# A sparse power-attention and expert layer on one core: relu sums on VectorE, expert tiles in two halves, and a new plan

## The chip, the core and the metric

The kernel runs on one core of a Trainium2 chip. The core has a matrix engine (TensorE, "PE" in the rows), a vector engine (VectorE, "DVE"), an activation engine (ScalarE, "ACT"), a general engine (GpSimd, "POOL") and a queue engine that issues transfers (SyncE, "SP"). TensorE writes its results into PSUM, which has 8 banks of 128 x 512 float32; VectorE and ScalarE read them from there, GpSimd does not. The metric is the device time of one execution in microseconds; the median of several executions counts.

## What is computed

The input x has 4 sequences of 1024 tokens with 128 channels. All arithmetic is in float32.

```
xn = layernorm(x)
out = x + attention(xn) + experts(xn)

attention:  q, k, v = split(xn @ W_attn + b_attn)        # 16 heads of 8
            s = q k^T;  s = s - mean(s over all keys)
            s = s / (mean |s| over all keys + 1e-6) * gain
            r = max(s where key <= query else -1000, 0) ** 4
            y = (r / (sum r + 1e-6)) v;  out = y @ W_proj + b_proj
experts:    two best of 8 experts per token (softmax of their two gate logits)
            h = (x w1 + b1) * (x w2 + b2);  g = silu(h wg + bg);  y = g w3 + b3
```

The mean of |s| runs over all 1024 keys, the fourth power over the causal ones only.

## The kernel before, in words

**Attention.** Each sequence is cut into two chunks of 512 queries (c = 0, 1); the 16 heads are taken in 4 groups of 4 (r). Matmuls of 4 heads run side by side in four 32-row or 32-column strips of the array. For the mean of |s|, `up` (L942) scores queries against keys to the right, and DVE (L955) or ACT (L957) adds up absolute values, one bank each. For the attention proper, `score` (L1066) writes scores of one block of 128 keys against 512 queries into 4 banks, one for each head. Then a relu on ACT (L1092) or DVE (L1094) moves each bank into an SBUF tile `u1`; a block on the diagonal is first masked by DVE (L1085). Two squarings (L1117 on ACT, L1119 on POOL, 1024 wide for two heads) make the fourth power in `u`. TensorE takes two products of them into one accumulator bank: `relus` (L1133) with the constant selector `pick`, which adds up the relus over the keys (with that sum, and the sum of all signed scores, the absolute values over the causal keys are found without a second pass), and `values` (L1142) with the values V and a column of ones. A sequence's second chunk has 4 whole blocks of keys ahead of its diagonal groups, the first chunk has none.

**Experts.** Token copies are scattered by an indirect transfer on POOL's queue (L723) into rows of a table `xs`, sorted by expert and padded to tiles of TS = 256 rows: 39 tiles. For each tile SP loads its rows and the weights of its expert (L1234 to L1238, 640 KB of weights), TensorE transposes the rows (L1247), multiplies by w1 and w2 (L1257), wg (L1264) and w3 (L1273); ACT adds the first bias (L1331) and takes the silu (L1363), DVE multiplies the two halves (L1339) and weights the result (L1285), and POOL adds the rows to a table in memory by an indirect transfer (L1293), 128 rows each.

**The order.** Every engine executes a fixed list. A planner in the kernel (`Plan.run`) makes the lists: each step has an engine or a choice of engines with a cost in microseconds, the steps it depends on, the buffers it takes and gives back, and a due time (`rank`). It takes the step that can start first, after shifts by name (`SOONER`, `RANK`). Where it foresees TensorE idle for over 0.3 us while an accumulator is open, it puts in a filler matmul of zeros (`pads`, emitted at L1426).

Buffers of note: 8 PSUM banks, 6 tiles `u1`, 8 tiles `u`, 14 tiles `blk` of 1040 columns, 2 weight tiles `w`, 3 row tiles `xg`.

Of the kernel before, what the change touches and what calls it, by code (L numbers as in the profile page):

```python
# [8 lines left out]
F32 = mybir.dt.float32  # L9
# [7 lines left out]
P = 128  # L17
# [6 lines left out]
CH = 512  # L24
VE = D + 2
VW = NH * VE + 22
TS = 256
# [24 lines left out]
class Plan:  # L52
# [6 lines left out]
    SOONER = {"score": 0.23, "mask": 0.1, "norm": 0.19, "tbias": -0.09, "count": -0.58, "v": 0.01, "top": 0.2, "wT": -0.06, "kappa": -0.11, "gateT": 0.12, "k": 0.21, "abs": -0.69, "ys": -0.51, "stats": 0.59, "exp": 0.14, "sq": -0.86, "bound": 0.53, "proj": -0.42, "least": 1.02, "xg": -0.51, "give": -0.32, "yT": -0.16, "sum": -0.3, "heads": 0.32, "gate": -0.5, "headsT": 0.15, "normal": 0.19, "second": -0.02, "relu": -0.88, "y@DVE": -0.32, "gate@DVE": 0.11, "relu@DVE": 0.45, "xT": 0.46, "xg@DVE": -0.05, "relu@ACT": 0.42, "out": -0.77, "yT@DVE": -0.19, "xT@DVE": -0.19, "place": -0.11, "gate@ACT": -0.01, "g": -0.01, "wT@ACT": 0.34, "heads@DVE": -0.33, "mean": -0.33, "y": -0.03, "abs@DVE": 0.6, "ys@DVE": -0.15, "sq@ACT": -0.11, "warm": 0.63, "xg@ACT": -0.83, "norm@ACT": 0.05, "up": 0.16, "q": 0.06, "blocks": -0.09, "ys@ACT": 0.01, "spill": -0.53, "weight": -0.46, "wT@DVE": 0.22, "gain": -0.07, "gates": 0.91, "av": -0.1}  # L59
    RANK = {"score": 221, "proj": -10, "yT": -194, "xg": -11, "sums": 48, "h": -24, "tbias": -35, "bound": -15, "top": 4, "headsT": 187, "spill": 12, "blocks": 240, "place": 4, "sum": -136, "std": -27, "gateT": 10, "count": -34, "scatter": 85, "xT": 210, "y": 196, "exp": 27, "second": -251, "load": 209, "relu": -111, "keys": 126, "mask": 6, "rows": -13, "scale": 8, "turn": 101, "wT": 23, "fill": 17, "ys": -19, "bias": -6, "g": -103, "give": -106, "gate": 36, "absq": 16, "norm": -137, "warm": -16, "v": -15, "hot": -162, "gates": 21, "stats": 20, "up": 78}  # L60
# [105 lines left out]
def layer_kernel(  # L166
# [49 lines left out]
    SB = TS // P  # L216
    N_TILES = (2 * NT + E * (TS - 1)) // TS
# [10 lines left out]
    def keep(shape, name, dtype=F32):  # L228
# [5 lines left out]
        "u": (8, [P, 2, CH]), "u1": (6, [P, 2, CH]), "blk": (14, [P, TB * WX]),  # L234
        "w": (2, [P, 2 * F + FB * F + FB * C]), "xg": (3, [P, SB, WX]), "xT": (2, [P, TS]),
        "z": (2, [P, FB, TS]), "s": (2, [P, FB, TS]), "ye": (2, [P, SB, C]),         "ys": (2, [P, CH]), "yt": (2, [P, CB, C]),
# [105 lines left out]
    tiles_f = keep([P, N_TILES], "tiles_f")  # L342
    expert_f = keep([P, 1], "expert_f")
    for t, pattern, base, cm in (
        (first, [[-1, E]], E, 0),
        (tiles_f, [[1, N_TILES]], 0, 0), (expert_f, [[0, 1]], 0, 1),
    ):
        nc.gpsimd.iota(t, pattern=pattern, base=base, channel_multiplier=cm, allow_small_or_imprecise_dtypes=True)
# [24 lines left out]
    xs = dram.tile([N_TILES * TS, WX], F32, name="xs")  # L373
# [47 lines left out]
    own = keep([E, N_TILES], "own")  # L421
    one8 = keep([P, TB], "one8")
    nc.vector.memset(one8, 1.0)
    owner = keep([P, N_TILES], "owner", I32)
    biases = keep([P, 3, FB, N_TILES], "biases")
# [130 lines left out]
    def route(rank):  # L556
# [84 lines left out]
        def owners(e):  # L641

            past = room(0, N_TILES * (E - 1)).rearrange("p (n e) -> p n e", e=E - 1)
            nc.vector.tensor_tensor(
                past, tiles_f.unsqueeze(2).to_broadcast([P, N_TILES, E - 1]),
                ends(1)[:, 1:].unsqueeze(1).to_broadcast([P, N_TILES, E - 1]), ALU.is_ge,
            )
            o0 = of_buf(k1)[:, NE + 160 : NE + 160 + N_TILES]
            nc.vector.tensor_reduce(o0, past, AX.X, ALU.add)
            nc.vector.tensor_copy(owner, o0)  # L650
            nc.vector.tensor_scalar(own, o0[:E, :], expert_f[:E, :], None, ALU.is_equal)
# [8 lines left out]
        def bias(e):  # L660
            pb = of_buf(k2)[:, : 3 * FB * N_TILES].rearrange("p (i f n) -> p i f n", i=3, f=FB)
            for i in range(3):
# [7 lines left out]
                biases.rearrange("p i f n -> p (i f n)"), of_buf(k2)[:, : 3 * FB * N_TILES]  # L670
# [72 lines left out]
    def prepare(b, cs, rank):  # L743
# [65 lines left out]
        def scale(here, bound):  # L809


            t = of_buf(aq)[:, here]
            nc.vector.tensor_scalar(
                t.bitcast(I32), bound.bitcast(I32), 0x7F800000, -0x1000000, ALU.bitwise_xor, ALU.bitwise_and
            )
            nc.vector.tensor_tensor(of_buf(qb)[:, here], of_buf(qb)[:, here], t, ALU.mult)  # L816

        sd = []
        for c in range(NC):
# [12 lines left out]
                    deps=[m, qd[c]], give=[k], rank=rank,  # L832
# [76 lines left out]
        m = add("heads", {"PE": 1.3}, heads, deps=sd + [bl], take=[sh[b]], give=[aq], rank=rank + 8)  # L909
# [10 lines left out]
    def chunk(b, c, vd, sh_done, t0, t1):  # L920
# [124 lines left out]
        for r in range(NR):  # L1045
            acc = Buf("bank")
            for j, grp in enumerate(groups):
# [29 lines left out]
                for m in range(2):  # L1077
                    u1, u = u1s[m], us[m]
                    a = []
                    for g in range(2):  # L1080
# [21 lines left out]
                        if rest:  # L1102
# [3 lines left out]
                                    give=[] if near else [k], rank=rank - 200,  # L1106
# [31 lines left out]
                def values(e, r=r, parts=parts, us=us, acc=acc, begin=False, end=False):  # L1138
# [8 lines left out]
                line["sq"] = sq1  # L1147

# [4 lines left out]
                    emit=lambda e, f=relus, s=begin and not diag: f(e, begin=s), deps=e1, took=took(counted), give=[],  # L1153
                    free=(u1s, e2), last=None, take=[acc] if begin and not diag else [],
                )
                av_job = dict(
                    acc=acc,
                    emit=lambda e, f=values, s=begin and diag, t=last: f(e, begin=s, end=t), deps=e2 + vd, took=took(w),
                    give=us, free=None, last=(r, acc) if last else None, take=[acc] if begin and diag else [],
                )  # L1160
                if begin and diag:
                    now, later = pending, [av_job, relu_job]
                else:
                    now, later = pending + ([relu_job] if counted else []), [av_job]
                    if not counted:
                        add("free", {"none": 0.0}, None, deps=e2, give=u1s)
# [48 lines left out]
    def experts(routed, ranks, stored):  # L1215
# [3 lines left out]
        tile_ = [{k: Buf(k) for k in ("w", "xg", "xT", "z", "s", "ye")} for _ in range(n_)]  # L1219

        def weights_of(i):
            w = of_buf(tile_[i]["w"])
# [4 lines left out]
        def loaded(i):  # L1227


            def load(e):  # L1230
                of_ = nc.sync.value_load(owner[0:1, i : i + 1], min_val=0, max_val=E - 1)
                this = bass.DynSlice(of_, 1)
                w1s, w2s, wgs, w3s = weights_of(i)
                nc.sync.dma_start(of_buf(tile_[i]["xg"]), slots_d[:, i * SB : (i + 1) * SB, :])  # L1234
                nc.sync.dma_start(w1s, w1[this, :, :].rearrange("e p f -> p (e f)"))
                nc.sync.dma_start(w2s, w2[this, :, :].rearrange("e p f -> p (e f)"))
                nc.sync.dma_start(wgs, wg[this, :, :].rearrange("e (k p) g -> p (e k) g", p=P))
                nc.sync.dma_start(w3s, w3[this, :, :].rearrange("e (k p) h -> p (e k) h", p=P))  # L1238

            return add(  # L1240
# [218 lines left out]
```

## Time and profile before

| | |
|---|---|
| median of 3 runs | 931.68 us (931.22 to 932.55) |
| profiled execution, its own time | 934.0 us |
| its span, first to last instruction | 932.3 us |
| mean granted TensorE clock | 0.985 |
| longest groups on TensorE (busy) | L942 188.4 us, L1066 178.9 us, L1142 165.1 us, L1133 129.1 us |
| experts on TensorE (busy) | L1264 77.1 us, L1257 74.7 us, L1273 44.9 us |
| first and last w1/w2 matmul (L1257) starts | 282.0 us; the last of L1273 at 906.5 us |
| moved by transfers | 58.63 MB, of it 117 loads of 128 KB and 39 of 256 KB for expert weights |

In a row of instruction groups, the part behind "x" is the count, then come busy time in us, the mean duration of one in ns, and the idle time of the engine ahead of them with what ended it. A float32 matmul shows as two instructions. Durations of one instruction contain the tail that the next one of the same engine overlaps, so the distance from start to start is shorter than the duration when instructions follow each other closely. In a timeline row the first number is the start, the second how long the merged group lasted.

### The profile page before, as it was taken

What the parts mean: (1) busy time and instruction counts of PE and PEld (TensorE: products, weight loads), DVE (VectorE), ACT (ScalarE), POOL (GpSimd) and SP (SyncE); (2) the same over time, 40 slices, a digit from 0 to 9 for tenths busy, and PEclk for the clock granted to TensorE, in tenths of its full rate; (3) what the DMA queues carried; (4) which work ended last, traced back from release to release, by engine and by line L of the source; (5) the groups of instructions that cost most, each with busy time, mean ns of one, the idle gap of its engine ahead of it and who ended that gap; (6) DMA issues with size and microseconds to landing.
All of it is one profiled execution on the core that took longest, in us unless ns stands there. A gap on an engine that the chain in (4) does not pass through costs nothing.

```text
span 932.3 us, 20608 instructions
## 1 busy us (share of the span) xinstructions
PE 901.4 (97%) x7517; PEld 458.4 (49%) x7517; DVE 644.5 (69%) x1616; ACT 718.1 (77%) x1564; POOL 756.1 (81%) x519
## 2 busy tenths in 40 slices
PE   6899999998999999999899999999999999999996
PEld 4455433433454545545445654454545565544443
DVE  7888856568776766666567776665666776666565
ACT  5879888897786868678757877777787868678983
POOL 4478879889676889999957887999987838899992
PEclk9999999999898999999989999999999999999999
DMA  4820000000021233233212221232322222222106
GB/s 107 333 79 22 24 21 21 22 24 21 22 80 39 48 76 78 58 68 78 63 41 54 67 57 43 60 65 59 83 63 63 56 62 59 63 59 44 41 7 187
DMA packets 66275, 58.63 MB, mean 63 GB/s; under 512 B 6463, under 2 KB 62206, under 8 KB 66174
## 3 DMA queue, kind: packets, MB, share of 16 engines
q1 hardware_dynamic: 52168, 47.67, 16.8%
q0 software_dynamic: 13280, 9.38, 7.4%
q8 instruction: 59, 0.97, 0.4%
q10 hardware_dynamic: 726, 0.27, 0.2%
q14 instruction: 42, 0.34, 0.1%
HBM read 36.90 MB, written 20.40 MB: 61 GB/s over the span
## 4 chain that ended last, share of the span: by engine, by line
PE 83%; DVE 7%; POOL 6%; issue 2%; DMA 1%; ACT 1%; SPq 0%; ACTq 0%; POOLq 0%; DVEq 0%
PE bank L942 17%; PE bank L1066 16%; PE bank L1142 14%; PE bank L1133 9%; PE bank L1264 8%; PE bank L1257 7%; PE bank L1273 4%; POOL u L1119 4%; PE bank L1010 2%; POOL xs L723 1%; PE bank L767 1%; PE bank L1247 1%; DVE blk L816 1%; PE bank L1426 1%; DMA blk<-acc 1%
## 5 line engine op out<-in xcount | busy, mean ns | idle before, releaser
L1119 POOL TENSOR_TENSOR u<-u 128x1024 f32<-128x1024 f32 (+1 forms) x324 | 582.1, 1924 | 99.4 <-ACT u L1092 62.7
L1117 ACT ACTIVATE u<-u 128x1024 f32<-128x1024 f32 (+1 forms) x316 | 298.2, 971 | 11.7 <-POOL u L1119 5.6
L955 DVE TENSOR_REDUCE asum<-bank 128x1 f32<-128x512 f32 (+3 forms) x500 | 243.0, 543 | 62.1 <-PE bank L942 61.3
L1092 ACT ACTIVATE u<-bank 128x256 f32<-128x256 f32 (+2 forms) x355 | 152.4, 492 | 71.9 <-DVE u L1085 44.0
L942 PE MATMUL bank<-blk,blk 32*128 32x512 f32 (+3 forms) x1536 | 188.4, 529 | 7.1 <-DVE blk L816 4.7
L1085 DVE SCALAR_TENSOR_TENSOR u<-bank,causal 128x256 f32<-128x256 f32 (+1 forms) x384 | 121.2, 372 | 89.6 <-PE bank L1066 70.9
L1066 PE MATMUL bank<-blk,blk 32*128 32x512 f32 (+3 forms) x1536 | 178.9, 528 | 1.0 <-DVE u L1085 0.5
L1142 PE MATMUL bank<-u,V 128*32 128x512 f32 (+3 forms) x1536 | 165.1, 501 | 1.6 <-POOL u L1119 1.3
L957 ACT ACTIVATE bank<-bank 128x512 f32<-128x512 f32 (+3 forms) x268 | 130.5, 488 | 35.1 <-PE bank L942 31.8
L1293 POOL DMA_INDIRECT acc<-ye,xg x78 | 123.0, 1577 | 36.6 <-DVE ye L1285 20.5
L1094 DVE TENSOR_SCALAR u<-bank 128x512 f32<-128x512 f32 (+2 forms) x157 | 98.9, 656 | 55.9 <-PE bank L1066 55.9
L942 PEld LDWEIGHTS bank<-blk,blk 32*128 32x128 f32 x1536 | 90.6, 185 | 86.1 <-issue 13.5
L1133 PE MATMUL bank<-u,pick 128*32 128x512 f32 (+3 forms) x1280 | 129.1, 469 | 0.0
L1066 PEld LDWEIGHTS bank<-blk,blk 32*128 32x128 f32 x1536 | 65.7, 184 | 72.5 <-issue 27.1
L1133 PEld LDWEIGHTS bank<-u,pick 128*32 128x32 f32 x1280 | 43.6, 111 | 79.3 <-issue 74.5
L723 POOL DMA_INDIRECT xs<-blk,slot x64 | 64.5, 1008 | 21.4 <-DMA xs<-blk,slot 11.2
L1264 PE MATMUL bank<-z,w 128*128 128x256 f32 x312 | 77.1, 390 | 0.0
L1142 PEld LDWEIGHTS bank<-u,V 128*32 128x32 f32 x1536 | 33.9, 108 | 83.4 <-issue 58.3
L1257 PE MATMUL bank<-xT,w 128*128 128x256 f32 x312 | 74.7, 383 | 0.0
L1264 PEld LDWEIGHTS bank<-z,w 128*128 128x128 f32 x312 | 56.1, 190 | 25.9 <-issue 8.8
L1257 PEld LDWEIGHTS bank<-xT,w 128*128 128x128 f32 x312 | 56.9, 193 | 7.7 <-DVE asum L955 1.5
L1339 DVE SCALAR_TENSOR_TENSOR z<-bank,biases,z 128x256 f32<-128x256 f32 x78 | 37.2, 478 | 30.8 <-ACT z L1331 30.7
(176 smaller groups left out, 700.5 us busy)
## 6 DMA issues: line engine op xcount, KB each, us to landing
w<-in_L_ffn_w_dram SPq DMA_DIRECT2D x117, 128.0 KB
w<-in_L_ffn_wg_dram SPq DMA_DIRECT2D x39, 256.0 KB
xs<-w SPq DMA_DIRECT2D x1, 5070.0 KB
xg<-xs SPq DMA_DIRECT2D x39, 130.0 KB
acc<-w SPq DMA_DIRECT2D x1, 2048.0 KB
blk<-acc SPq DMA_DIRECT2D x4, 512.0 KB
out_dram<-xt SPq DMA_DIRECT2D x8, 256.0 KB
xt<-in_L_attn_x_dram SPq DMA_DIRECT2D x3, 512.0 KB
```

The lines of the kernel that those rows point to most:

```text
L942: nc.tensor.matmul(of_buf(ks_[g])[:, at : at + w], of_buf(q[b])[rows_, ii * P : (ii + 1) * P], of_buf(km[b][r])[rows_, k0 : k0 + w], start ...
L955: nc.vector.tensor_reduce(to, of_, AX.X, ALU.add, apply_absolute_value=True)
L957: nc.scalar.activation(of_, of_, AF.Abs, accum_out=to)
L1066: nc.tensor.matmul(of_buf(ks_[g])[:, at : at + n], of_buf(km[b][r])[rows_, jj * P : (jj + 1) * P], of_buf(q[b])[rows_, c * CH + off : (c + ...
L1092: nc.scalar.activation(to, s_, AF.Relu)
L1117: nc.scalar.activation(to, s_, AF.Square)
L1119: (nc.vector if e == "DVE" else nc.gpsimd).tensor_tensor(to, s_, s_, ALU.mult)
L1133: nc.tensor.matmul(of_buf(acc)[32 * g : 32 * g + 32, off + lo : CH], pick, of_buf(u1s[g // 2])[:, g % 2, at + lo : at + n], start=begin, s ...
L1142: nc.tensor.matmul(of_buf(acc)[32 * g : 32 * g + 32, off:CH], of_buf(Vb[b])[:, jj, h0 : h0 + 32], of_buf(us[g // 2])[:, g % 2, at : at + n ...
L1257: nc.tensor.matmul(of_buf(k)[:, j * TS : (j + 1) * TS], wt[:, f * P : (f + 1) * P], of_buf(tile_[i]["xT"]), start=True, stop=True)
L1264: nc.tensor.matmul(of_buf(k)[:, g * TS : (g + 1) * TS], weights_of(i)[2][:, f, g * P : (g + 1) * P], of_buf(tile_[i]["z"])[:, f, :], start ...
L1293: nc.gpsimd.indirect_dma_start(out=acc_d, in_=of_buf(ye)[:, j, :], in_offset=None, compute_op=ALU.add, out_offset=bass.IndirectOffsetOnAxi ...
```

## The change

1. In a second chunk, the relus of the whole key blocks are not summed by TensorE block by block. The first block's relus stay in `u1`; for the second to fourth block VectorE reads the score bank again and adds max(score, 0) to a running sum in SBUF (`more`, a scalar_tensor_tensor of 512 columns for each of 4 heads). After the fourth block one `pick` product of the sums takes the place of four. Relu and `more` of one bank are separate steps, and the bank comes free after both. The accumulator is now begun by the values product.
2. Expert slots are padded to 128 rows (TS = 128), 72 halves in all, and two halves, each with its own expert, make one tile: 36 tiles. Matmuls by weights have 128 moving columns each; biases, product and silu are done half by half; each half loads its own 640 KB.
3. The rows of a tile are loaded by a step of their own (`rows_in`), apart from the weights (`load`). Transposing waits for the rows alone, the w1/w2 products also for the weights.
4. In the preparation of a sequence, the power-of-two scale is computed inside the PSUM bank, the queries are multiplied by it from there, and a copy step puts it into SBUF for later use.
5. `SOONER` and `RANK` have new values, `w` has 4 tiles, `blk` 11.

```diff
-TS = 256
+TS = 128
...
-    SB = TS // P
-    N_TILES = (2 * NT + E * (TS - 1)) // TS
+    SB = 2
+    TW = SB * TS
+    N_TILES = -(-((2 * NT + E * (TS - 1)) // TS) // SB)
+    N_OWN = N_TILES * SB
...
-        "u": (8, [P, 2, CH]), "u1": (6, [P, 2, CH]), "blk": (14, [P, TB * WX]),
-        "w": (2, [P, 2 * F + FB * F + FB * C]), "xg": (3, [P, SB, WX]), "xT": (2, [P, TS]),
+        "u": (8, [P, 2, CH]), "u1": (6, [P, 2, CH]), "blk": (11, [P, TB * WX]),
+        "w": (4, [P, 2 * F + FB * F + FB * C]), "xg": (3, [P, SB, WX]), "xT": (2, [P, TW]),
...
-            t = of_buf(aq)[:, here]
-            nc.vector.tensor_scalar(
-                t.bitcast(I32), bound.bitcast(I32), 0x7F800000, -0x1000000, ALU.bitwise_xor, ALU.bitwise_and
-            )
-            nc.vector.tensor_tensor(of_buf(qb)[:, here], of_buf(qb)[:, here], t, ALU.mult)
+            t = bound.bitcast(I32)
+            nc.vector.tensor_scalar(t, t, 0x7F800000, -0x1000000, ALU.bitwise_xor, ALU.bitwise_and)
+            nc.vector.tensor_tensor(of_buf(qb)[:, here], of_buf(qb)[:, here], bound, ALU.mult)
...
+                if not diag and j:
+                    for m in range(2):
+                        for g in range(2):
+                            k = ks_[2 * m + g]
+
+                            def more(e, m=m, g=g, k=k, first=j == 1, before=relus_0, sums=sums):
+                                to = of_buf(sums[m])[:, g * CH : (g + 1) * CH]
+                                nc.vector.scalar_tensor_tensor(
+                                    to, of_buf(k), 0.0, of_buf(before[m])[:, g, :] if first else to, ALU.max, ALU.add
+                                )
+
+                            a = add(
+                                "more", {"DVE": t_dve(CH)}, more, deps=[scores] + (before_ if j == 1 else [added[2 * m + g]]),
+                                take=[sums[m]] if j == 1 and g == 0 else [], rank=rank - 200,
+                                behind=[added[2 * m]] if j == 1 and g else [],
+                            )
+                            add("free", {"none": 0.0}, None, deps=[a, e1[2 * m + g]], give=[k])
...
+                if not diag:
+                    def all_relus(e, sums=sums, acc=acc):
+                        for g in range(4):
+                            nc.tensor.matmul(
+                                of_buf(acc)[32 * g : 32 * g + 32, :], pick, of_buf(sums[g // 2])[:, (g % 2) * CH : (g % 2 + 1) * CH],
+                                start=False, stop=False,
+                            )
+
+                    relu_job = None
+                    if j == c * CB - 1:
+                        relu_job = dict(acc=acc, emit=lambda e, f=all_relus: f(e), deps=list(added), took=took(CH), give=sums, free=None, last=None, take=[])
...
+            def rows_(e):
+                nc.sync.dma_start(of_buf(tile_[i]["xg"]), slots_d[:, i * SB : (i + 1) * SB, :])
...
+                for j in range(SB):
+                    n = i * SB + j
+                    of_ = nc.sync.value_load(owner[0:1, n : n + 1], min_val=0, max_val=E - 1)
...
         def up(i, f, k):
-            for j, wt in enumerate(weights_of(i)[:2]):
-                nc.tensor.matmul(
-                    of_buf(k)[:, j * TS : (j + 1) * TS], wt[:, f * P : (f + 1) * P], of_buf(tile_[i]["xT"]), start=True, stop=True
-                )
+            for m in range(2):
+                for j in range(SB):
+                    nc.tensor.matmul(
+                        of_buf(k)[:, m * TW + j * TS : m * TW + (j + 1) * TS], weights_of(i, j)[m][:, f * P : (f + 1) * P],
+                        of_buf(tile_[i]["xT"])[:, j * TS : (j + 1) * TS], start=True, stop=True,
+                    )
```

## The prediction, made before the changed kernel ran

> **What bounds the kernel now.** I read the busy times first, then the groups by form, TensorE's timeline, the waits, and the busy times by stage.
>
> ```profile
> PE 901.4 (97%) x7517; PEld 458.4 (49%) x7517; DVE 644.5 (69%) x1616; ACT 718.1 (77%) x1564; POOL 756.1 (81%) x519
> ```
>
> TensorE is busy for all but 31 us of 932.3; no other engine passes 81%. The chain of work that ended last is 83% PE. So work taken off TensorE should pay, as long as no other engine takes its place. The timeline of a second chunk (start, length) gives the price of a burst of 8 instructions as distance from start to start:
>
> ```profile
> 407.62 1.16 PE L1273 MATMUL bank<-w,s 128*128 128x128 f32 x8
> 408.61 1.89 PE L1257 MATMUL bank<-xT,w 128*128 128x256 f32 x8
> 410.43 0.71 PE L942 MATMUL bank<-blk,blk 32*128 32x256 f32 x8
> 411.08 1.07 PE L1142 MATMUL bank<-u,V 128*32 128x512 f32 x8
> 411.96 1.04 PE L1133 MATMUL bank<-u,pick 128*32 128x512 f32 x8
> 412.93 1.14 PE L942 MATMUL bank<-blk,blk 32*128 32x512 f32 x8
> ```
>
> A values burst followed by a selector burst lasts 0.88 us (411.08 to 411.96); the selector burst, followed by a burst of another kind, 0.97. The groups by form give the vector side:
>
> ```profile
> L1117 ACT ACTIVATE u<-u 128x1024 f32<-128x1024 f32 x253 | 261.8, 1057 | 8.5 <-POOL u L1119 5.4 <-DVE u L1094 2.3
> ...
> L957 ACT ACTIVATE bank<-bank 128x512 f32<-128x512 f32 x143 | 84.1, 588 | 21.3 <-PE bank L942 20.9
> L1094 DVE TENSOR_SCALAR u<-bank 128x512 f32<-128x512 f32 x126 | 82.4, 685 | 55.9 <-PE bank L1066 55.9
> ...
> L1092 ACT ACTIVATE u<-bank 128x512 f32<-128x512 f32 x130 | 70.6, 595 | 23.4 <-PE bank L1066 23.0
> ```
>
> A relu of 512 takes 595 ns on ACT, 685 on DVE. Two squares in a row last 1.99 us on ACT in the timeline, so each is started 0.11 us before its predecessor's tail ends: a queued ACT instruction costs its mean less 0.11 us.
>
> **The change on TensorE.** Per sequence and head group, 4 selector bursts of whole blocks become 1. There are 4 x 4 such pairs: 48 bursts fewer. The switch to the next kind of burst (0.09) stays, so each saves 0.88: **-42 us**, all on the engine that is never idle.
>
> Experts: a tile costs 1.82 (L1257) + 1.8 (L1264) + 0.99 (L1273) + 0.32 (transposes, by the same timeline) = 4.95 us, x39 = 193. Now w1/w2 and wg take 16 instructions of 128 columns each for 8 of 256. L1273 is that shape: 8 in 0.99, with the switch to it; 16 cost at most 1.98, and 1.88 if the switch of about 0.1 is paid once. With 1.88: 5.07 x 36 = 183; with 1.98: 5.27 x 36 = 190. So -10 to -3; I take **-9**, since the 16 are one burst. Here the Trainium skill speaks against the change: "TensorE: Matmul & The Clock Gate", Back-to-back issue gap, gives about 81 ns a matmul for a sustained stream of weight load and 128 columns, as the weights are not free; a float32 instruction being two passes (0.216 us for 256 columns here), that is 162 ns each, 2.6 us a burst, and 36 x 2 x 0.7 = 50 us more. The row L1273 has a fresh 128x128 weight load for every instruction and still runs at 0.124 us; it decides.
>
> Filler matmuls: the order of the changed kernel has 33 of them for 17, with 9 instead of 1 of 512 columns. By the rows of L1426 (0.83 us for one of 384, 0.6 of 256) that is about 24 us for 12: **+12**. Where the wait that they fill is real, they cost nothing more, but then the wait does.
>
> The scale: its product of two SBUF operands (L816) takes 1638 ns, one of a PSUM and an SBUF operand (L1208, 128x512) 686. TensorE waited for it 4.7 us in all; I take **-3** (0 to -5). The new copy into SBUF feeds only `heads`, off the path: 8 x 0.68 us of DVE.
>
> Sum for TensorE: 932.3 - 42 - 9 + 12 - 3 = 890.
>
> **The change on ACT.** Counts from the order of both kernels, each at its queued price: 1024-wide squares 253 to 283, +30 x 0.95 = 28; 512-wide 63 to 69, +3; relus of 512 130 to 240, +110 x 0.485 = 53; of 384 99 to 124, +10; absolute sums (L957 and its accumulator read, 0.61 from start to start at 512) 268 to 321, +26; expert biases and silus: 156 of 256 columns become 288 of 128, about 0.33 + 0.26 a pair for 0.44, +17; normalizing +4. Sum +141: ACT goes from 718 to about **858 us** busy. The planner moved relus to ACT because DVE now has the sums. A part of the 718 is tails of instructions that nothing followed; with a queue that never empties I get about 820 as the lower end. This is the largest engine load of the changed kernel beside TensorE's, and the profile of before never ran ACT above 87% in a stage (51.76 of the 60 us from 60 on).
>
> A wait is added too. `more` on DVE and relu on ACT read the same bank, and the program lets one wait for the other: 142 of 192 sums wait for ACT, 57 of 240 relus for DVE (none of 130 before). The nearest row is the mask and relu of one bank:
>
> ```profile
> DVE u L1085 <- PE bank L1066: 70.9, 69, 3.1
> ...
> ACT u L1092 <- DVE u L1085: 44.0, 50, 2.6
> ```
>
> 168 relus had such a wait in the program, 44.0 us idle, 0.26 each; for 57 that is 15 us, and 0.6 each (a whole sum ahead) 34. Behind a waiting relu stand ACT's squares and absolute sums, so banks come back later and `up` and `score` wait. I take **+20**. Without the cover of a full queue it is idle time of ACT, not hidden. "PSUM — Partial Sum Buffer", PSUM bank collisions raise a hardware error, says that two engines must not touch one bank at once, reads included: the planner's two free steps can't overlap on a bank.
>
> **Beside other work.** DVE: +192 sums at 0.61 to 0.69 (L1094; the sum also reads SBUF like L1085, 417 ns at 256) = +125, relus 126 to 16 and 29 to a few -87, absolute sums -26, products +6: about 660 of 644, under the cover of 25% idle. POOL: 36 squares less (-66), 6 row transfers less (L1293, 1577 ns: -9): 680. Transfers: expert weights 25.6 to 47.2 MB.
>
> ```profile
> 0.00:25.00 25.00, 17.42 (x86) 11.50 (x86) 18.74 (x101) 14.24 (x37) 11.21 (x42) 1.00 0.39 100
> ...
> 296.00:470.00 174.00, 168.36 (x1379) 88.79 (x1379) 114.95 (x265) 128.32 (x262) 159.33 (x94) 0.99 0.29 65
> ...
> 890.00:932.00 42.00, 33.68 (x296) 17.38 (x288) 25.11 (x62) 24.90 (x59) 24.20 (x14) 0.96 0.38 107
> ```
>
> (PE, PEld, DVE, ACT, POOL busy, clock, DMA share, GB/s.) At 65 GB/s the transfers take 0.29 of the engines in the expert stage; doubling the weights gives about 0.55. SP issues one every 0.58 us, so a tile's 8 take 5 us and land some 9 us after the start, in a period of (906 - 282)/36 = 17 us: hidden. Rows ahead of weights: 0. If the weights came late, each late us would count up to 36 times. Fewer `blk` and the `u1` pair held through the second block: 0, at worst some waits of `score`.
>
> **The rivals.**
> (a) *ACT and TensorE share the bound* (forecast). ACT outside the middle: 11 us idle in the first 25 and 17 in the last 42. 858 + 28 + 20 = 906; TensorE's own 890. Two fixed lists coupled by 8 banks lose a little at each other; a full ACT queue gives tails back (up to -38). I put the span at 911, from 899 to 927. For it: every price is a row. Against it: ACT would be busy 94%.
> (b) *TensorE alone*: ACT runs in TensorE's shadow, span 890, 883 to 898. For it: 97% busy before. Against: ACT's 858.
> (c) *ACT becomes the bound, and slower.* Mechanism: relus, sums and squares of a second chunk all pass ACT in a fixed order, waiting in turn for PE, DVE and POOL. The busiest row of an engine other than PE is POOL's 159.33 of 174, 92%. If ACT can't do better in the middle, with 39 us of its work in head and tail: (858 - 39)/0.92 + 67 = 957; with tails given back, (830 - 39)/0.92 + 67 = 927. From a busy share of 94.5% of the middle downward at 858 the change loses: (858 - 39)/0.945 + 67 = 934. Range 934 to 965.
> (d) *It does nothing*: gains and ACT's waits cancel, 930 to 934.
>
> **How the numbers follow.** The profiled execution took 934.0, 1.7 over its span, and 2.3 over the median of the runs: 911 + 1.7 - 2.3 = **911**, to the nearest. Chances: (a) 0.54, (b) 0.13, (c) 0.28, (d) 0.05. The bound for no change is 0.2%, about what runs of this kernel can tell (929.8 to 933.5): faster 0.68, same 0.04, slower 0.28. The range leaves out the fastest of (b) and the worse half of (c): 886 to 946; (a) by itself is 898 to 927.
>
> **What would show it.** Right: selector instructions of 512 columns 512 to 128; L1273's successors at 0.11 to 0.125 us an instruction; ACT busy 830 to 870, above DVE and POOL; new waits of ACT's relus for the sums and of the sums for ACT; PE idle or waiting more than 31 us. Wrong: ACT under 800 busy; PE under 840 with a longer span; 128-column bursts at 2.6 us; SP's weights late and `h` waiting for a transfer; the sums at 1.6 us like L816.

## The result, and the profile after

The changed kernel takes 947.34 us (median of 4 runs, 946.62 to 948.58); the kernel before took 931.58 us beside it. The ratio is 1.0169, with a 95% interval of 1.0151 to 1.0187: slower, where 911 us and faster were forecast. The profiled execution took 946.62 us.

The page after, to be read against the rows of before in the prediction (the first of each engine's figures is its busy time in us):

```profile
span 944.9 us, 21806 instructions
...
PE 907.5 (96%) x7663; PEld 501.2 (53%) x7663; DVE 659.7 (70%) x1694; ACT 837.6 (89%) x1965; POOL 684.5 (72%) x477
```

The loads of ACT, DVE and POOL are near the forecast (858, 660, 680). TensorE is the surprise: 890 was forecast, and it is busier than before, although it has less to do. The groups by form, after:

```profile
L1125 ACT ACTIVATE u<-u 128x1024 f32<-128x1024 f32 x283 | 296.8, 1079 | 1.4 <-POOL u L1127 0.9 <-DVE u L1093 0.4
L948 PE MATMUL bank<-blk,blk 32*128 32x512 f32 x768 | 147.6, 658 | 2.8 <-ACT u L1100 1.3 <-DVE blk L1163 0.5 <-ACT bank L963 0.3
...
L1074 PE MATMUL bank<-blk,blk 32*128 32x512 f32 x768 | 130.0, 654 | 0.5 <-DVE blk L816 0.5
L1100 ACT ACTIVATE u<-bank 128x512 f32<-128x512 f32 x240 | 127.7, 613 | 23.5 <-DVE blk L1163 19.3 <-PE bank L1074 3.1
...
L1163 DVE SCALAR_TENSOR_TENSOR blk<-bank,blk 128x512 f32<-128x512 f32 x128 | 82.9, 684 | 25.8 <-ACT u L1100 21.3 <-PE bank L1074 4.3
...
L1190 PE MATMUL bank<-blk,pick 128*32 128x512 f32 x128 | 16.7, 592 | 0.0
```

The same answer for the kernel before had these three groups at 512 columns:

```profile
L942 PE MATMUL bank<-blk,blk 32*128 32x512 f32 x768 | 127.5, 650 | 6.6 <-DVE blk L816 4.7 <-DVE u L1085 2.0
...
L1066 PE MATMUL bank<-blk,blk 32*128 32x512 f32 x768 | 112.6, 641 | 0.3 <-DVE blk L816 0.3
...
L1133 PE MATMUL bank<-u,pick 128*32 128x512 f32 x512 | 68.7, 593 | 0.0
```

The selector's 512 instructions of 512 columns are 128 (now L1190): 68.7 us became 16.7, as announced. But `up` (L942, now L948) and `score` (L1066, now L1074) have the same 768 instructions each, at nearly the same mean duration, and are busy 37.5 us longer. Over all their forms they went from 367.3 to 416.3 us, +49.0, against -55.0 for all selector products together (129.1 to 57.4 and 16.7). Their instructions overlap less, they stand farther apart. TensorE's timeline shows it at one place (start, length in us; PEld is TensorE loading the fixed operand of its next matmuls, the bracket how long that load waited and for whom):

```profile
139.05 1.14 PE L1074 MATMUL bank<-blk,blk 32*128 32x512 f32 x8
140.12 1.01 PE L1150 MATMUL bank<-u,V 128*32 128x256 f32 x8
141.06 1.78 PE L1074 MATMUL bank<-blk,blk 32*128 32x512 f32 x8
142.95 9.29 PE L948 MATMUL bank<-blk,blk 32*128 32x512 f32 x32
```

```profile
141.72 0.29 PEld L1074 LDWEIGHTS bank<-blk,blk 32*128 32x128 f32 x2 [0.35 <-DVE blk L1163]
...
144.16 0.29 PEld L948 LDWEIGHTS bank<-blk,blk 32*128 32x128 f32 x2 [0.92 <-DVE blk L1163]
...
146.05 0.50 PEld L948 LDWEIGHTS bank<-blk,blk 32*128 32x128 f32 x4 [0.99 <-ACT u L1100]
```

The same 8 instructions take 1.14 us and then 1.78, and 32 take 9.29 where four times 1.14 would be 4.6, at full clock up to 145.6 us and at half clock from there. Inside these bursts the loads wait for a sum (L1163) or a relu (L1100) to be done with a bank. Such a wait is written as busy, not as idle: from 142.20 to 145.60 us TensorE is busy for 3.21 of 3.40 us with 10 instructions, in the 3.40 us before that with 35. By the records, 28.7 us of the 416.3 lie in stretches of half clock, and 11.8 of the 367.3 before, so some 8 us of the 49.0 are the clock (half of the difference, an estimate). Of the waits between sums and relus, the changed kernel has (us in total, times, longest):

```profile
DVE blk L1163 <- ACT u L1100: 39.8, 51, 2.8
```

The sums on DVE wait 39.8 us for relus on ACT, and ACT's relus wait 19.3 us for sums (in the row of L1100 above). Neither wait was there before. The stages show a second thing, before and then after, in busy us of PE, PEld, DVE, ACT, POOL, then the granted clock, the DMA share and GB/s:

```profile
0.00:300.00 300.00, 283.11 (x2241) 133.41 (x2245) 222.60 (x606) 241.03 (x524) 225.38 (x203) 0.97 0.19 63
300.00:600.00 300.00, 294.86 (x2504) 155.52 (x2500) 203.46 (x479) 225.49 (x499) 256.07 (x154) 0.99 0.27 60
```

```profile
0.00:300.00 300.00, 275.59 (x2125) 130.63 (x2129) 225.03 (x604) 258.36 (x573) 215.94 (x197) 0.93 0.17 56
300.00:600.00 300.00, 297.20 (x2609) 175.60 (x2600) 201.84 (x503) 272.33 (x662) 220.76 (x134) 0.99 0.38 96
```

In the first 300 us the changed kernel runs 116 matmul instructions fewer, on a clock of 0.93 for 0.97. Of these, 96 are selector instructions that the change takes out, so its attention is no further than before (480 instructions of `score` for 500, 552 of `up` for 536) although it had less to do, and none of the experts' 36 has run. Its first token copies are scattered at 89.5 us for 68.1 and its first w1/w2 matmul runs at 311.1 us for 284.9 (the 282.0 of the table above is the queue's wait ahead of it). So there were three suspects: banks with two readers, the late start of the experts (11 `blk` tiles for 14), and ACT's load. The order of the steps stands behind all three.

### The profile page after: what moved, and what is told of

Its sections match the earlier page's. It is cut to its first block, busy times and chain, and to the rows that moved or that the text cites. A ratio compares the mean times of both kernels' runs of the same rounds, so it can differ in the third digit from the quotient of the medians.

```text
span 944.9 us, 21806 instructions
## 1 busy us (share of the span) xinstructions
PE 907.5 (96%) x7663; PEld 501.2 (53%) x7663; DVE 659.7 (70%) x1694; ACT 837.6 (89%) x1965; POOL 684.5 (72%) x477
## 4 chain that ended last, share of the span: by engine, by line
PE 71%; ACT 17%; DVE 8%; issue 2%; POOL 1%; DMA 0%; DVEq 0%; ACTq 0%
PE bank L948 17%; PE bank L1074 14%; PE bank L1150 12%; PE bank L1326 7%; ACT u L1125 6%; ACT u L1100 6%; PE bank L1317 6%; PE bank L1141 3%; PE bank L1335 3%; ACT bank L963 2%; DVE blk L1163 2%; PE bank L1016 2%; PE bank L1491 1%; PE bank L1190 1%; PE bank L769 1%
## 5 line engine op out<-in xcount | busy, mean ns | idle before, releaser
L1127 POOL TENSOR_TENSOR u<-u 128x1024 f32<-128x1024 f32 (+1 forms) x288 | 519.4, 1932 | 124.1 <-ACT u L1100 65.3
L1125 ACT ACTIVATE u<-u 128x1024 f32<-128x1024 f32 (+1 forms) x352 | 336.9, 992 | 1.5 <-POOL u L1127 0.9
L1100 ACT ACTIVATE u<-bank 128x512 f32<-128x512 f32 (+2 forms) x490 | 220.5, 528 | 49.5 <-DVE blk L1163 19.3
L948 PE MATMUL bank<-blk,blk 32*128 32x512 f32 (+3 forms) x1536 | 212.0, 536 | 3.1 <-ACT u L1100 1.3
L1074 PE MATMUL bank<-blk,blk 32*128 32x512 f32 (+3 forms) x1536 | 204.3, 538 | 4.1 <-DVE u L1093 2.3
L948 PEld LDWEIGHTS bank<-blk,blk 32*128 32x128 f32 x1536 | 108.8, 188 | 77.0 <-issue 13.9
L1074 PEld LDWEIGHTS bank<-blk,blk 32*128 32x128 f32 x1536 | 82.8, 186 | 70.7 <-issue 24.5
L1163 DVE SCALAR_TENSOR_TENSOR blk<-bank,blk 128x512 f32<-128x512 f32 x128 | 82.9, 684 | 25.8 <-ACT u L1100 21.3
L1401 DVE SCALAR_TENSOR_TENSOR z<-bank,biases,z 128x128 f32<-128x128 f32 x144 | 43.6, 345 | 49.1 <-ACT z L1394 41.3
L1326 PE MATMUL bank<-z,w 128*128 128x128 f32 x576 | 74.2, 281 | 0.2
L1317 PE MATMUL bank<-xT,w 128*128 128x128 f32 x576 | 70.8, 276 | 0.0
L963 ACT ACTIVATION_READ_ACCUMULATOR bank<-bank 128x1 f32 x321 | 66.1, 206 | 0.0
L1163 DVE SCALAR_TENSOR_TENSOR blk<-bank,u 128x512 f32<-128x512 f32 x64 | 41.9, 687 | 24.3 <-ACT u L1100 18.5
```

The lines of the kernel that those rows point to most:

```text
L948: nc.tensor.matmul(of_buf(ks_[g])[:, at : at + w], of_buf(q[b])[rows_, ii * P : (ii + 1) * P], of_buf(km[b][r])[rows_, k0 : k0 + w], start ...
L963: nc.scalar.activation(of_, of_, AF.Abs, accum_out=to)
L1074: nc.tensor.matmul(of_buf(ks_[g])[:, at : at + n], of_buf(km[b][r])[rows_, jj * P : (jj + 1) * P], of_buf(q[b])[rows_, c * CH + off : (c + ...
L1100: nc.scalar.activation(to, s_, AF.Relu)
L1125: nc.scalar.activation(to, s_, AF.Square)
L1127: (nc.vector if e == "DVE" else nc.gpsimd).tensor_tensor(to, s_, s_, ALU.mult)
```

## The experiments

Each time stands beside the kernel before in the same session, and its ratio is to that. "The same order" means that the planner's order is unchanged.

**Is TensorE's work the end?** The kernel before in the same order, without the selector bursts of its second to fourth whole block; these relus are left out of the normalizing sum.

```diff
-def relus(e, parts=parts, ..., begin=False):
+def relus(e, parts=parts, ..., begin=False, none=j > 0 and not diag):
+    if none:
+        return
```

> The kernel before, in its own order, with the selector bursts of the second to fourth whole block left out and nothing in their place (those relu sums are missing from the normalization). If TensorE is the bound of before and what its bursts cost is what they are worth, 48 x 0.88 us go: about 890 us. If TensorE's busy time in before already holds waits for banks that VectorE and ScalarE release, only part comes through: 905 to 925.

921.66 us, ratio 0.9901 (0.9863 to 0.9939). Its page:

```profile
PE 869.9 (95%) x7133; PEld 451.9 (49%) x7133; DVE 648.0 (71%) x1616; ACT 714.9 (78%) x1564; POOL 756.6 (82%) x519
```

All 48 bursts gone, with no work put elsewhere, give 11 us, not 42. TensorE is busy 31.5 us less (901.4 to 869.9) and idle 17.5 us more (30.9 to 48.4): another engine's result is late next (`values` idles 6.5 us for POOL's squares, 1.3 before; `score` 4.9 for ACT's relus, 0.2 before). But `up` and `score` together grow only from 367.3 to 372.7 us. Their +49.0 in the changed kernel is thus not what follows whenever other bursts go. This is the ceiling of the change's main gain in the order that before had.

**Is ACT's list, or DVE's, the end?** The changed kernel in the same order with ACT's second squares at half width (half of these fourth powers are not computed), and with the sums of the third and fourth block at 64 columns (the rest is not added).

```diff
-s_, to = of_buf(src)[:, :, :w], of_buf(dst)[:, :, :w]
+n = w // 2 if e == "ACT" and src is dst else w
+s_, to = of_buf(src)[:, :, :n], of_buf(dst)[:, :, :n]
```

```diff
-to = of_buf(sums[m])[:, g * CH : (g + 1) * CH]
+n = CH if first else 64
+to = of_buf(sums[m])[:, g * CH : g * CH + n]
...
-to, of_buf(k), 0.0, ...
+to, of_buf(k)[:, :n], 0.0, ...
```

> The changed kernel, in its own order, with the second squares that ScalarE takes done on half of their columns only (the other half stays a square instead of a fourth power): 189 instructions, some 73 us less ScalarE work, everything else as it is. Theory 1 (ScalarE's list is the bound, 837.6 us busy): the time falls by more than half of that, to 890 to 910. Theory 2 (TensorE is still the bound, the sums hold its banks longer): it falls by less than 12 us, to 935 to 947. Theory 3 (the experts start late because routing starts late): the first w1/w2 matmul stays at about 311 us and the time falls by less than 15 us.

> The changed kernel, in its own order, with the relu sums of the third and fourth block cut to 64 columns (the rest of those sums is missing): 128 instructions of 0.15 for 0.61 us, some 60 us less VectorE work, the same waits between sums and relus. Theory 1 (ScalarE's list): only the waits of relus behind whole sums get shorter (19.3 us idle in all), so 930 to 945. Theory 2 (banks held by the sums): banks of two blocks in three come back 0.5 us earlier each, so 905 to 925.

Half squares: 940.58 us, ratio 1.0094 (1.0065 to 1.0123), with ACT's load down by 63 us:

```profile
PE 895.3 (96%) x7663; PEld 492.8 (53%) x7663; DVE 659.6 (70%) x1694; ACT 774.9 (83%) x1965; POOL 683.8 (73%) x477
```

Short sums: 936.9 us, ratio 1.0047 (1.0031 to 1.0063), with DVE 51 us lighter. So 63 us on ACT buy 7, and 51 us on DVE, which is only 70% busy, buy 10. The theory that ACT is the bound falls: half squares end far above its 890 to 910, with the first w1/w2 matmul at 310.7 us as before. Short sums missed the 905 to 925 us of the theory of held banks and lie in the other range; that banks come back earlier fits their 10 us, but is not shown by it. The length of the sums' wait is not the cost: with short sums it is longer (54.6 us for 39.8), while ACT's relus wait less for sums (10.9 for 19.3).

**Fillers and transfers.** The changed kernel without its 33 filler matmuls, and with the weights of a tile's second half not loaded (the first half's weights serve both).

```diff
-if n.pad:
+if False and n.pad:
```

```diff
-for j in range(SB):
+for j in range(1):
...
-w = of_buf(tile_[i]["w"][j])
+w = of_buf(tile_[i]["w"][0])
```

> The changed kernel in its own order without its 33 filler matmuls (23 us of TensorE by their rows). If they delay real work, the time falls by 10 to 20 us. If they only fill waits, it stays within 3 us; if they keep the clock up, it rises by up to 10 us with a lower granted clock.

> The changed kernel in its own order, with the weights of a tile's second half not loaded and the first half's weights used for both (wrong where the two experts differ): 23.6 MB and 144 + 144 transfers on SyncE less. If weight traffic or SyncE's list costs anything, it falls: 938 to 943 or lower. If it is hidden, as the forecast said: within 2 us of 947.

948.07 us (ratio 1.0168, 1.0140 to 1.0197) and 949.53 us (1.0179, 1.0147 to 1.0212): neither costs anything that these runs can tell, though the second lies 2.2 us above the changed kernel. Without fillers the mean clock of the profiled execution fell from 0.971 to 0.965.

**A try at freeing the banks.** In the same order, 139 of the 192 sums read the relu from `u1` in SBUF, where it was already there, instead of the bank.

```diff
-to, of_buf(k), 0.0, ...
+to, of_buf(u1)[:, g, :] if there else of_buf(k), 0.0, ...
```

> The changed kernel in its own order, but 139 of the 192 relu sums (all whose relu stands ahead of them in the order) read the relu in SBUF instead of the score bank, so that the bank is free after the relu alone and the sum's wait for ScalarE no longer keeps it. Theory 4 (what limits is how long the 8 banks are held; the sums are second readers that hold them): 935 to 941, about what cutting the sums to 64 columns gave. If sums of two SBUF operands take as long as the 1.6 us of the scale's product in the kernel before, VectorE gets 130 us more work: then 950 to 980. If the sums' place in VectorE's list alone matters: within 3 us of 947.

1046.48 us, ratio 1.1216 (1.1168 to 1.1265). The sums themselves became slow in the mean, so this says nothing on the banks:

```profile
L1168 DVE SCALAR_TENSOR_TENSOR blk<-u,blk 128x512 f32<-128x512 f32 x100 | 144.9, 1484 | 11.0 <-ACT u L1103 10.7
...
L1168 DVE SCALAR_TENSOR_TENSOR blk<-u,u 128x512 f32<-128x512 f32 x39 | 61.9, 1592 | 16.4 <-ACT u L1103 16.3
```

The means hide two kinds. Shortest, median and longest of the same instructions, in ns:

```profile
L1168 DVE SCALAR_TENSOR_TENSOR blk<-u,blk x100: 675/684/10595, 115.0 to 1012.3; 128x512 f32<-128x512 f32 x100
...
L1168 DVE SCALAR_TENSOR_TENSOR blk<-bank,blk x28: 674/681/692, 113.1 to 1009.4; 128x512 f32<-128x512 f32 x28
```

More than half of them are as fast as those that read a bank; some take many times as long. The last section says which.

**An order that knows of the shared bank.** The planner starts a step when its inputs and buffers are there. It does not know that relu and sum of one bank, which it holds for independent, cannot run together. This version tells it so, and `SOONER` and `RANK` were searched anew for the planner's own end. The control was searched without that knowledge. The steps are those of the changed kernel; the order, the fillers (28 with the knowledge, 33 without) and, for some steps, the engine differ.

```diff
+for b in n.reads:
+    start = max(start, reader.get(id(b), 0.0))
...
+for b in n.reads:
+    reader[id(b)] = max(reader.get(id(b), 0.0), end + self.HOP)
...
+a.reads, e1[2 * m + g].reads = [k], [k]
```

> The changed kernel with another order of the same instructions: the planner now counts that ScalarE's relu and VectorE's sum of one bank cannot read it together, and its tables were searched anew. If the loss comes from banks shared by two readers in an order that does not know of it, most of the 15.8 us go: 925 to 935 us. If the sums cost by themselves whatever the order, or if the fewer work tiles do (still 11), it stays at 942 to 950 us.

> The changed kernel with its tables searched anew by the same search as the order that counts shared banks, but not counting them. If the exclusive banks are the cause, it stays where the changed kernel is or goes beyond: 940 to 955 us. If any new search finds the same 12 us, 930 to 938 us, and the shared banks are not shown to be it.

(In the last line `a` is the sum and `e1[...]` the relu of bank `k`.) Knowing: 935.56 us, ratio 1.0032 (1.0014 to 1.0049). Not knowing: 950.79 us, ratio 1.0199 (1.0165 to 1.0234). In the waits, first of the order that knows (its L1167 and L1104 are L1163 and L1100), then of the other:

```profile
DVE blk L1167 <- ACT u L1104: 1.4, 5, 0.6
```

```profile
DVE blk L1163 <- ACT u L1100: 39.3, 47, 3.2
```

The wait of 39 us is gone, the other way round it fell from 17.0 to 0.2, and 1.67% of 932, about 15.6 us, come back. TensorE's busy time is 888.6 for 911.2 us. The control is not a worse plan by the planner's own measure: the latest end in its list is 919.2 us without the knowledge and 920.6 with it. So in this pair nearly the whole loss lies in the order. It does not follow that the sums are free once the planner knows: `up` and `score` are busy 402.0 us here, 415.2 in the control and 367.3 before.

**Does the late routing count?** The same with the normalized rows of sequences 1 to 3 in the weight tiles, which lie idle then; the order was searched anew for it.

```diff
-t = xn[b] = Buf("blk")
+t = xn[b] = Buf("w" if b else "blk")
```

> The whole change with shared banks counted in the order, and in addition the normalized rows of sequences 1 to 3 put into the tiles of the experts' weights, which lie idle then, so that the 11 work tiles are not short when the routing is worked out. If the late routing still costs in the order that counts shared banks (935.6 us): 922 to 931 us, with the first scatter about 15 us earlier. If it does not: 933 to 940 us.

935.82 us, ratio 1.0030 (1.0011 to 1.0048). The first scatter came at 75.6 us for 86.8, the first w1/w2 product at 290.5 for 299.1, and the time is the same. An earlier start of the experts gained nothing here that was not lost elsewhere.

**The parts alone**, each searched anew: sums alone (whole tiles of 256, 14 `blk`, shared banks known), halves alone (selector bursts as before, 11 `blk`), and the kernel before as a control. Both parts keep the new place of the scale.

```diff
-TS = 128
+TS = 256
...
-"blk": (11, [P, TB * WX]),
+"blk": (14, [P, TB * WX]),
```

That is the core of the first, with the expert functions of before. The second takes the loop over key groups, with its relus and selector bursts, from before:

```diff
-give=[] if near or (j and not diag) else [k], rank=rank - 200,
+give=[] if near else [k], rank=rank - 200,
```

The control differs from before in the values of `SOONER` and `RANK` alone.

> Sums alone: expert slots in whole tiles of 256 and 14 work tiles as before, order searched anew with the shared banks counted. If the late routing by fewer work tiles is most of the loss, this is faster than before: 905 to 920 us. If the freed TensorE time is not what sets the end, and the sums just pay for themselves: 925 to 935 us. If the sums cost in any order: 940 us or more.

> Halves alone: 128 expert slots, rows loaded apart and 11 work tiles, the selector bursts of before (no sums), order searched anew. If the halves bring their 9 us of TensorE's work and the work tiles cost nothing: 920 to 926 us. If the 11 work tiles delay the routing by 20 us at any order: 932 to 945 us.

> Control: the kernel before with its tables searched anew by the same search. If a search by itself is worth something, 925 us or less; if the order of before was as good as the search finds, 929 to 934 us.

Sums alone 927.43 us, ratio 0.9934 (0.9911 to 0.9956); halves alone 941.14, ratio 1.0084 (1.0057 to 1.0112); control 939.84, ratio 1.0061 (1.0040 to 1.0083). A new search by itself made before 6 us slower, so an order's luck is at least of that size, and 6 us between two orders prove little. Against the control, sums gain 1.3% and halves nothing, by one order each.

**The planner's span.** The earliest time of an expert tile is spread over a constant, `SPAN = 930`: tile 35 of 36 is not planned before 60 + 848.5 x 35/36 = 885 us, however short the rest has become. With 900 it is 857 us, with 870 it is 830; the other due times shrink along. Searched anew with that:

```diff
-SPAN, BEGIN = 930.0, 25.0
+SPAN, BEGIN = 900.0, 25.0
```

> Halves alone, searched anew with the planner's own span, from which the expert tiles get their earliest times, set to 900 instead of 930. If those fixed earliest times hold back what the shorter TensorE work could bring: 925 to 934 us, 8 us or more below the 941.1 us of halves alone. If the end is set by work on the chip and not by the due times: 937 to 945 us.

> Halves alone with span 900 once more, from another search that began elsewhere, so that the order is another one: if 920.3 us was the luck of one order, this lies 8 us or more above; if the span did it, 916 to 926 us.

> Halves alone with the planner's span set to 870. If the earliest times still hold back at 900: 911 to 917 us. If TensorE's list is the end there (890.8 us busy in a span of 918.5 at 900): 918 to 926 us.

> Sums alone with shared banks counted, the planner's span set to 900 instead of 930. If the earliest times hold back the freed TensorE time: 915 to 923 us. If not: 925 to 932 us, as sums alone did with 930.

> Control: the kernel before, order searched anew, with the planner's span 900 instead of 930 and nothing else. If the gain of 20 us that the span brought the halves comes from the earliest times alone: 918 to 926 us here too. If it needs the halves' shorter TensorE work: 930 to 942 us.

> The whole change with shared banks counted and the planner's span 900. If due times held back the 50 us that sums and halves free on TensorE: 915 to 925 us, faster than before. If banks and ScalarE's load set the end: 931 to 942 us, as with 930 (935.6 us).

| kernel | 930 | 900 | other |
|---|---|---|---|
| halves alone | 941.14, 1.0084 | 920.26, 0.9868 (0.9843 to 0.9892) | 900, another order: 928.93, 0.9968 (0.9955 to 0.9982); 870: 920.33, 0.9887 (0.9860 to 0.9915) |
| sums alone | 927.43, 0.9934 | 941.83, 1.0091 (1.0057 to 1.0124) | |
| before, searched anew | 939.84, 1.0061 | 942.33, 1.0125 (1.0108 to 1.0142) | |
| whole change, shared banks known | 935.56, 1.0032 | 922.71, 0.9903 (0.9886 to 0.9921) | |

All three orders of halves with an earlier span beat the one with 930, by 12 to 21 us. The kernel before gains nothing by it, and sums alone lost 14, against both theories; that is not explained. So an earlier span helped two of four kernels, and that it needs shorter work is a guess. The whole change gains 13 and is now faster than before by 1.0%. Its first w1/w2 product starts at 288.7 us for 299.1, so most of this gain is there before the experts begin; how it divides between due times and the search was not separated. Halves alone at 900 are at least as fast, without any sum on DVE:

```profile
PE 890.8 (97%) x8009; PEld 475.7 (52%) x8009; DVE 629.3 (69%) x1665; ACT 739.0 (80%) x1714; POOL 745.6 (81%) x513
```

**All orders side by side.** The planner's end is the latest end of a step in the list that it makes, so it is fixed before the kernel runs. The last column is the busy time of `up` and `score` together in the profiled execution. All in us.

| kernel, order | planner's end | time | over it by | `up` + `score` |
|---|---|---|---|---|
| before | 926.5 | 931.6 | 5.1 | 367.3 |
| before, searched anew: 930; 900 | 924.9; 919.7 | 939.8; 942.3 | 15.0; 22.7 | 362.2; 362.4 |
| halves: 930; 900; 900, another; 870 | 919.0; 908.6; 906.0; 902.5 | 941.1; 920.3; 928.9; 920.3 | 22.2; 11.7; 22.9; 17.8 | 369.3; 372.4; 366.4; 369.8 |
| sums, banks counted: 930; 900 | 924.7; 920.1 | 927.4; 941.8 | 2.7; 21.8 | 389.7; 384.6 |
| whole, banks counted: 930; rows in `w`; 900 | 920.6; 919.2; 913.1 | 935.6; 935.8; 922.7 | 15.0; 16.6; 9.6 | 402.0; 390.9; 397.5 |
| whole, not counted: as changed; searched anew | 919.3; 919.2 | 947.3; 950.8 | 28.1; 31.6 | 416.3; 415.2 |

Two things stand out. The two orders with sums that do not count shared banks exceed their plan by more than any other; but the others scatter by 20 us too, also without any sum, so the share of luck in one pair is large. And without sums `up` and `score` take 362 to 373 us in every order; with sums 385 to 402 where the banks are counted, and 415 to 416 where they are not. So the sums come with longer bursts elsewhere on TensorE in every order found here, by 17 us at the least against before.

**The clock, a thread through all of these.** Span times (1 - clock) is 14.0 us before (932.3 x 0.015) and 27.4 after (944.9 x 0.029): the difference, 13.4, is as large as that of the spans, 12.6. The other end is halves at 900, 918.5 x 0.008 = 7.3. Yet the clock alone is not the loss: the order that counts shared banks has nearly the clock of the changed kernel (0.973 for 0.971) and is 12 us faster. Within one kernel a lower clock goes with a longer time: in the 86 executions of before that stand beside these runs (clock 0.978 to 0.992), 4.4 us for 0.01 in the mean. By that the 0.014 between before and after would be some 6 us, an estimate; which of the two brings the other on, it does not tell. The row of granted clock in 40 slices, after:

```profile
PEclk9899898898999999999999999999999999999997
```

But for the last, the low slices lie in the first 260 us. The Trainium skill, "TensorE: Matmul & The Clock Gate", A second HAM failure mode, tells, of a bfloat16 kernel, of matmul groups cycling through PSUM banks whose short pauses make the clock swing between half and full. The trace agrees in kind: the clock is at half in stretches of 3.4 or 6.8 us, one begins at 220.7 us inside a TensorE pause of 4.3 us that ACT's result ended, but another, at 145.6 us, has no visible pause ahead of it, only the 3.40 us with 10 instructions for 35. If it is so, a stall costs twice, once as a wait and again as half speed; no run here shows it, as none kept the clock up through the same waits.

## Why the prediction was wrong

**Failed: "-42 us, all on the engine that is never idle".** This term of TensorE's sum took a busy share of 97% for TensorE's own work, with nothing behind it. Two things were found instead. Taking the same bursts out of before, with nothing in their place, gave 11: 17.5 us came back as idle time, because other engines' results were late next. And with the sums in the kernel, `up` and `score`, which the forecast left as they were, grew by 49.0 us, against 55.0 less on the selectors. The growth comes with the sums: without them it is 5.4 us at most in any order, with them 17 to 35 even where the planner counts the shared banks. That it is time spent waiting for banks is what the loads inside the bursts show (0.92 us for a sum, 0.99 for a relu); how much of the 49.0 is that was not added up.

**Failed: "Two fixed lists coupled by 8 banks lose a little at each other".** The sum put this at 5 us (906 to 911). The time came out 36 us above that. About 15 of these came back in the one pair of orders that differ in whether the planner counts the two exclusive readers of a bank. The prediction saw the wait (142 of 192 sums) and even that the planner holds the two steps for free. It priced only ACT's side: +20, and ACT's own wait was 19.3. The other side it left under the cover of DVE's 25% idle time. But the bank is held while the two readers go one after the other, and TensorE's next burst needs the bank; idle time of DVE does not shorten that. The sums' own wait of 39.8 us is not the price of it, since the kernel with short sums waits longer there and is faster.

**Not refuted: "Fewer `blk` ...: 0, at worst some waits of `score`".** The experts began 26 us later in the changed kernel, but the tiles are not shown to be the reason: with 11 of them the first w1/w2 product starts at 286.8 us (halves, 900) and 288.7 (whole change, 900), with 14 at 293.0 (sums alone). With the tiles eased and the shared banks known, the time did not move. In the changed kernel's own order it was not tried.

**Not asked at all:** whether the planner could use shorter work. Its earliest times, fixed for 930, were in the code; with an earlier span halves were 12 to 21 us and the whole change 13 us faster, though the other two kernels were not.

**Rival (c)** named the right side and 934 to 965 us. Its formula even fits: ACT reached (838 - 39)/(945 - 67) = 91% outside head and tail, below the 94.5% named as the turning point. But that share is only another way of writing the span. Its mechanism, ACT's list as the bound, fell: 63 us less on ACT gave 7. So its number came near by luck.

**Right.** The sums cost 684 and 687 ns, not 1.6 us (forecast 0.61 to 0.69 us). The experts' matmuls fell by 10.6 us of busy time (211.9 to 201.3 with the transposes; forecast 9). A burst of 16 instructions of 128 columns takes 1.88 us from start to start, as taken, and not 2.6; in TensorE's timeline:

```profile
422.01 1.95 PE L1317 MATMUL bank<-xT,w 128*128 128x128 f32 x16
423.89 0.71 PE L1074 MATMUL bank<-blk,blk 32*128 32x256 f32 x8
```

ACT's 837.6 lies inside 820 to 858. Transfers are hidden. The power-of-two scale fell from 1638 to 688 ns in the mean, and TensorE's wait for it from 5.0 to 0.5 us (forecast 3 less). But 1638 was the mean of five products of 691 to 693 ns and three of 2731 to 4174, not the price of one. **Mis-sized:** the fillers, +12 in the sum, cost nothing, as they stand in real waits.

**Open:** how the loss divides between waits and clock, how much of it is the luck of one order, why sums alone got slower with the earlier span, and whether a better order of the whole change would come near 911; the best one found takes 922.7.

## What to carry to other kernels

A TensorE that is busy 97% in bursts that cycle through PSUM banks may be waiting inside its busy time: before counting on freed matmuls, leave them out of the kernel as it is and see how many of their microseconds come through (here 11 of 42). The number of instructions in a stretch, and the waits of the weight loads, show what the busy time hides. A second reader of a bank is not free on an idle engine: here the matmul bursts that fill the banks took 17 us more and upward with it, in every order. A planner that makes the order has to be told that two readers exclude each other; that was worth 15 us of 951 in one pair of orders. Look for due times that still hold the old length when work gets shorter. And judge by more than one order: two that the planner put within 3 us of each other lay 6 to 9 us apart on the chip.

## What the runs showed of the hardware

Where both operands of a VectorE sum of 512 columns lie in SBUF, its time hangs on what GpSimd does. In the kernel in which 139 sums read the relu from SBUF, 67 ran with no GpSimd square beside them, by start and end of the records, and took 675 to 727 ns each. The other 72 took 2290 ns in the mean and 10595 at most. The 53 sums of that kernel that read a bank took 674 to 692 ns, 43 of them beside a square. The scale's product of before shows the same two kinds:

```profile
L816 DVE TENSOR_TENSOR blk<-blk,blk x8: 691/693/4174, 32.4 to 695.4; 128x512 f32<-128x512 f32 x8
```

The Trainium skill, "SBUF — State Buffer", Who interferes with whom, gives a reason that agrees: a VectorE instruction with two SBUF inputs takes its second one through a read port that it shares with GpSimd, and so contends with a GpSimd instruction that reads SBUF. The second reading of the bank, which makes the two readers exclude each other, is thus the cheaper way here, by 0.8 us a sum in the mean.
